# Values by Strassen's scheme, small steps of norms and attention on other engines, and a new order of work in a two-layer graph network

## The chip, the cores and the metric

The kernel runs on one core of a Trainium2 chip. The core has five engines that work side by side, each through its own queue of instructions in order: TensorE (PE; matrix products, loading its weights as PEld), VectorE (DVE), ScalarE (ACT), GpSimd (POOL) and SyncE (SP), which issues the DMA transfers here. PSUM is the small memory that TensorE writes its products to, in eight banks; SBUF is the working memory. The metric is the time of one execution on the device, in microseconds (us), lower is better, as the median of several runs.

## What is computed

Input are 64 graphs of 256 nodes with 256 features (`x`) and an integer adjacency (`adj`, 0 or 1). Two layers run one after the other on every graph:

```python
# layer 0: attention with one set of values for each of R = 4 relations, 8 heads of 32
q, k = src @ Wq + bq, src @ Wk + bk
attn = softmax(q k^T / sqrt(32))                      # per head, 256 x 256
out  = sum over r of (attn * (adj == r)) @ (src @ Wv[r] + bv[r])
x = layernorm(src + out @ Wo + bo)
x = layernorm(x + gelu(x @ W1 + b1) @ W2 + b2)        # FF = 1024

# layer 1: two graph attentions with the same adjacency
def gat(h, W, a):
    Wh = h @ W
    e = leaky_relu(Wh @ a[:256] + (Wh @ a[256:])^T, 0.2)
    return softmax(where(adj > 0, e, NEG), axis=1) @ Wh
h = layernorm(x + gat(gat(x, W1, a1), W2, a2))
return layernorm(h + relu(h @ w_ff1 + b_ff1) @ w_ff2 + b_ff2)
```

All is in float32.

## The kernel before

One graph at a time is cut into 217 named steps, built by `Graph.operations`. A name is a stage and an index: `qk`, `s`, `max`, `exp`, `rec`, `nrm` are the scores and the softmax of layer 0 (index: half m of the features, head h); `eT`, `eW`, `eR` turn the softmax round with a transpose in blocks on VectorE, a write to DRAM and a read back; `ec` copies it to PSUM on ScalarE, `pm` and `pl` multiply it by the masks of the relations on VectorE and GpSimd, `po` multiplies by the values, `oT` copies the result out of PSUM on ScalarE, `wo` is the output product and `ya` its add. `a..` and `b..` are the feed-forward blocks of the two layers: `au`/`bu` the first product, `ax`/`bx` the activation, `aS`/`bS` differences of the hidden tile, `ad`/`bd` the second product, `ae`/`be` the adds of its parts to the residual, `ag`, `ar`, `bg`, `br` the residual's gain and offset. `st`, `rt`, `nb`, `ln`, `lg`, `lb` are statistics, inverse root, offset, application, gain and shift of the four layer norms. `ga`, `gac`, `ip`, `z`, `zl`, `zm`, `zx`, `ze`, `zd`, `h1`, `h1c`, `h2`, `h2a` are the two graph attentions A and B: `ip` spreads the left scores by a transpose on TensorE, `z` adds the right ones on ScalarE while it reads PSUM, `zl` is the leaky rectifier, `zm` the mask, `zx` the maximum, `ze` the exponential, `zd` scales the rows of Wh by the softmax's sums, `h1` and `h2` are the products, `h1c` and `h2a` their readers. `hT`, `hW`, `hR`, as `aT`, `aW`, `aR` and `bT`, `bW`, `bR`, turn an activation round by way of DRAM.

Each step has a number in `PLACES`, its place. Step n of graph g is emitted at `g * PERIOD + PLACES[n]`, with PERIOD = 60, and all steps of all graphs are sorted by that number. So the places set nothing but the order in which each engine gets its instructions: graphs overlap, some seven in flight (a graph's places run from 40 to 456). Taken modulo 60, the places give the order in a steady period. The loads of the weights and the preparation of the weights have places of their own (`LOAD_PLACE`, `FFA_PLACE` and so on).

The second products of the two feed-forward blocks are done by Strassen's scheme in Winograd's form: the 2 x 2 blocks of the hidden tile and of the weights give seven products in place of eight. The combined weights are made once, by `seven_weights`; the combined left sides are the `S` steps, on GpSimd.

The values of layer 0 are not: for each half m and each half jc of the nodes, `v_product` accumulates two matmuls (k = 0, 1) of 128 x 512 (four relations of 128) in PSUM, and `v_add` (line 496) adds the bias on VectorE. A float32 matmul shows as two records in the trace.

PSUM: one tag, `mm`, with two buffers, serves nearly all products (values, qk, first products, wo, po, ga, ip, h1, h2 and three of the second feed-forward products). A new one takes the buffer whose last reader stands first in the order. The other four second products share one bank, tag `po` of pool `ps_o`; access to the same bank of a tile is ordered as emitted, reads and writes of different blocks included. Four banks hold the scores (`s`), one the copied softmax (`pe`).

The steps that the change touches, by lines: `stats` with the epsilon (341), `root` (345), `offset` (349), `residual` with its four buffers, `v_product` (489), `v_add` (496), `gat_scores` (606), `gat_leaky` (610), `gat_divide` (628 the reciprocal, 630 the scaling). Around them stand `apply` (354), `plus` and `times` (324, 321), `heads_out` (557), `difference` (400), `down` (412), `add` (420), `maximum` (510), `exponential` (518), `normalise` (528), `masked` (540), `masked_last` (545) and `gat_maximum` (617).

Of the kernel before, what the change touches and what calls it, by code (L numbers as in the profile page):

```python
# [17 lines left out]
P = 128  # L18
S = 32
A = P // S  # L20
EPS = 1e-5
# [7 lines left out]
    "load": 40.36, "cast": 58.74, "xT": 60.44, "qk0": 70, "qkc0": 71.44, "qk1": 87.85, "s0": 89.53,  # L29
    "qkc1": 91.95, "max01": 94.22, "max03": 94.25, "max02": 94.39, "exp01": 95.36, "rec01": 97.24,  # L30
    "exp03": 106.64, "exp02": 109.12, "jT": 113.27, "max00": 114.1, "exp00": 118.89, "rec02": 119.85,
    "nrm01": 120.5, "rec00": 121.94, "mask0": 122.78, "rec03": 123.27, "eT01": 124.55, "s1": 124.66,
    "mask1": 124.91, "nrm02": 125.88, "max11": 126.34, "v00": 126.75, "nrm03": 126.97, "eT02": 128.02,
    "vc00": 128.34, "nrm00": 128.91, "eW01": 131.85, "eR01": 133.5, "mask2": 134.22, "max13": 137.47,
    "eT03": 137.69, "eW02": 138.09, "max10": 139.15, "exp13": 140.04, "max12": 141.09, "eR02": 141.63,
    "v01": 142.38, "exp11": 142.41, "eT00": 142.98, "exp12": 143.77, "rec11": 143.99, "exp10": 144.12,
    "vc01": 146.63, "rec12": 146.73, "mask3": 146.81, "rec10": 147.48, "nrm11": 148.13, "eW03": 148.24,
    "ec01": 149.05, "eW00": 151.36, "rec13": 152.13, "eT11": 152.55, "nrm12": 153.62, "nrm13": 153.65,
    "eR00": 153.67, "eT12": 155.05, "v10": 155.72, "eW11": 155.83, "y": 156.64, "pm01": 156.67,
    "vc10": 157.33, "ec00": 158.45, "pl00": 159.54, "pl02": 160.62, "pm00": 161.31, "eR03": 162.29,  # L40
    "nrm10": 163.21, "ec02": 163.47, "v11": 164.04, "vc11": 164.08, "mask4": 164.38, "pm02": 164.4,
    "pl01": 165.26, "ec03": 167.13, "eT10": 167.24, "eW12": 168.06, "eR11": 169.25, "pl03": 169.3,
    "pm03": 173.29, "eR12": 174.65, "eW10": 176.2, "eT13": 176.62, "eR10": 177.38, "po0": 181.21,
    "ec11": 181.79, "oT0": 183.85, "pm11": 184.85, "ec10": 187.85, "pl10": 187.87, "pl12": 191.61,
    "pm10": 191.97, "pl11": 192.4, "yb": 193.93, "eW13": 195.61, "eR13": 196.93, "ec12": 197.13,
    "pm12": 199.06, "pl13": 199.85, "ec13": 202.51, "pm13": 205.64, "po1": 215.6, "oT1": 217.97,
    "wo": 219.51, "ya": 223.88, "st1": 228.47, "rt1": 233.65, "nb1": 233.99, "ln1": 238.78, "aT": 240.73,
    "ag": 245.39, "aW": 246.11, "ar": 246.93, "aR": 249.98, "au0": 253.28, "ax0": 255.01, "au1": 255.12,
    "ax1": 256.29, "au2": 257.32, "au3": 258.21, "ax2": 258.83, "ax3": 259.91, "ad1": 260.54, "aS1": 262.22,
    "ae1": 262.56, "ad5": 262.62, "ad2": 263.26, "aS2": 263.54, "aS3": 264.31, "ad3": 264.44, "ad7": 265.04,  # L50
    "aS4": 265.78, "ad4": 265.92, "ad6": 267.49, "ae5": 269.57, "ae7": 270.4, "ae": 270.63, "ae6": 271.84,
    "st2": 272.17, "rt2": 272.17, "nb2": 273.67, "ln2": 274.48, "lg2": 276.04, "lb2": 279.25, "hT": 280.72,
    "hW": 284.48, "hR": 287.09, "ga0": 291.2, "ga1": 292.43, "gac0": 295.5, "gac1": 295.79, "ipA": 296.6,
    "zA": 298, "zlA": 298.97, "zmA": 299.01, "zxA": 299.7, "zeA": 303.47, "zdA": 304.35, "h10": 304.89,
    "h1c0": 305.16, "h11": 306.57, "h1c1": 306.58, "ipB": 307.84, "zB": 308.32, "zlB": 309.79,
    "zmB": 309.85, "zxB": 311.38, "zeB": 311.5, "zdB": 318.17, "h2": 319.09, "h2a": 319.31, "st3": 322.4,
    "rt3": 324.85, "nb3": 325.29, "ln3": 325.64, "bT": 326.01, "bW": 326.15, "bR": 335.32, "bu0": 339.02,
    "bg": 339.45, "bx0": 339.7, "br": 344.42, "bu1": 345.17, "bx1": 346.89, "bu2": 347.56, "bx2": 348.07,
    "bS1": 349.24, "bu3": 349.7, "bd1": 350.78, "bx3": 352.33, "bS2": 355.82, "bd2": 356.22, "bd5": 356.9,
    "bd3": 357.53, "bS4": 358.73, "bd4": 360.41, "be5": 361.74, "be": 361.79, "bS3": 367.41, "bd6": 368.29,  # L60
    "be1": 372.14, "be6": 374.71, "bd7": 376.99, "be7": 378.33, "st4": 407.09, "rt4": 408.17, "nb4": 413.39,
    "ln4": 428.85, "lg4": 434.13, "lb4": 437.94, "store": 455.81,
}
LOAD_PLACE, LOAD_STEP = 62.0, 3.0
FFA_PLACE, GAT_PLACE, FFB_PLACE = 196.0, 200.0, 252.0
# [14 lines left out]
def kernel(  # L80
# [110 lines left out]
    while loads:  # L191
        issue_load()
    scale = 1.0 / math.sqrt(DH)
# [49 lines left out]
    def seven_weights(b, t):  # L243


        nc.vector.tensor_tensor(t[0], b[0][1], b[1][1], ALU.add)
        nc.vector.tensor_tensor(t[1], t[0], b[0][0], ALU.subtract)
        nc.vector.tensor_tensor(t[2], b[1][0], t[1], ALU.subtract)
        nc.vector.tensor_tensor(b[0][1], b[0][0], b[0][1], ALU.subtract)
        return {1: b[0][0], 2: b[1][0], 3: t[2], 4: b[1][1], 5: t[0], 6: t[1], 7: b[0][1]}  # L250
# [525 lines left out]
```

## Time and profile before

| | us |
|---|---|
| median of 3 runs | 3729.13 (3727.47 to 3731.34) |
| the profiled execution | 3730.06 |
| its span, first to last instruction | 3728.3 |

| engine | busy us in the span | what it does |
|---|---|---|
| TensorE | 3525.8 | 25944 matmul records |
| VectorE | 3253.6 | 5652 instructions |
| GpSimd | 2683.8 | 2246 instructions |
| ScalarE | 2476.3 | 6661 instructions |

The granted clock of TensorE is full from about 200 us on, and 0.987 over the span. DMA queues move 457.93 MB, 123 GB/s.

How to read it: busy time of an engine is the time in which one of its instructions runs, and an instruction that is held up after its start counts as busy. A record of an instruction in the timeline has its start, its length, engine, line, operation, output and input tiles, shapes and count; in square brackets the idle time of the engine in front of it and what ended it. Since the engines take their instructions in order, a wait of one instruction delays everything behind it in its queue. The chain of waits goes back from the last instruction to what released it, and so on; its pieces are in order of time, with start and length.

### The profile page before, as it was taken

The numbers are of one execution on the slowest core, as the hardware profiler recorded it, in microseconds if no ns is written. First come the engines' busy times: TensorE is split into PE (matmuls) and PEld (weight loads), VectorE is DVE, ScalarE is ACT, GpSimd is POOL, SyncE is SP. The second block draws the span as 40 slices with busy tenths as digits, with TensorE's granted clock in tenths as the row PEclk, the third lists the DMA queues.
The fourth block names the chain that finished last, engine by engine and source line by source line (L and its number), as shares of the span: only waits on it lengthen the run. The fifth ranks groups of instructions, "written<-read, shape, count | busy, mean of one in ns | idle before, by whom it ended". The sixth has DMA issues, their size and how long they took to land.

```text
span 3728.3 us, 72927 instructions
## 1 busy us (share of the span) xinstructions
PE 3525.8 (95%) x25944; PEld 2739.0 (73%) x25944; DVE 3253.6 (87%) x5652; ACT 2476.3 (66%) x6661; POOL 2683.8 (72%) x2246
## 2 busy tenths in 40 slices
PE   5899999999999999999999999999999999999986
PEld 3577777777777777777777777777777777777775
DVE  4789999999999999999999999989989989989963
ACT  4667667667667666666666666666666666666642
POOL 2577777777777777777777777777777777777753
PEclk7999999999999999999999999999999999999998
DMA  6444444444444444444444444444444444444420
GB/s 176 123 127 123 120 132 123 121 131 124 122 131 124 122 131 124 122 131 124 122 131 124 122 129 124 124 128 124 124 128 124 125 128 123 126 128 123 120 77 29
DMA packets 809883, 457.93 MB, mean 123 GB/s; under 512 B 334256, under 2 KB 718896, under 8 KB 809520
## 3 DMA queue, kind: packets, MB, share of 16 engines
q1 hardware_dynamic: 809520, 453.27, 41.5%
q8 instruction: 206, 3.38, 0.4%
q14 instruction: 157, 1.29, 0.1%
HBM read 243.42 MB, written 201.33 MB: 119 GB/s over the span
## 4 chain that ended last, share of the span: by engine, by line
PE 77%; DVE 16%; ACT 2%; DMA 2%; issue 1%; SPq 1%; POOL 0%; ACTq 0%; POOLq 0%; DVEq 0%
PE po L557 12%; PE ffb_ps L377 11%; PE v_ps L489 9%; PE ffa_ps L377 6%; PE ffa_po L412 5%; PE ffb_po L412 5%; PE ffa_pq L412 5%; PE ffb_pq L412 4%; PE s L505 4%; PE h_ps L636 4%; PE ga_wps L587 3%; PE h_ps L650 3%; DVE pm L540 3%; PE qk_ps L470 3%; PE wo_ps L577 3%; DVE gb_z L610 3%
## 5 line engine op out<-in xcount | busy, mean ns | idle before, releaser
L540 DVE TENSOR_TENSOR pm<-rel,pe 128x1536 f32<-128x1536 uint8 x512 | 886.6, 1732 | 9.8 <-ACT pe L536 7.7
L545 POOL TENSOR_TENSOR pl<-rell,eT 128x512 f32<-128x512 bf16 x512 | 589.4, 1167 | 117.9 <-DMA eT<-eT_d 98.9
L345 POOL TENSOR_TENSOR rs_x<-ve_x,nhalf 128x2 f32<-128x2 f32 x256 | 182.5, 713 | 550.4 <-DVE ve_x L341 549.9
L489 PE MATMUL v_ps<-wv,xT 128*128 128x512 f32 x1024 | 491.3, 602 | 0.4 <-DVE v L496 0.4
L518 ACT ACTIVATE e<-s,nmax 128x256 f32<-128x256 f32 x1024 | 473.1, 477 | 20.8 <-DVE nmax L510 12.7
L377 PEld LDWEIGHTS ffb_ps<-ffb_T,f 128*128 128x128 f32 x2048 | 391.3, 191 | 121.6 <-issue 71.6
L377 PE MATMUL ffb_ps<-ffb_T,f 128*128 128x256 f32 x2048 | 466.7, 381 | 13.8 <-DMA ffb_T<-ffb_T_d 13.8
L377 PE MATMUL ffa_ps<-ffa_T,w 128*128 128x256 f32 x2048 | 466.5, 381 | 1.5 <-ACT ffa_h L385 1.5
L528 ACT ACTIVATE e<-e,rden 128x256 f32<-128x256 f32 x1024 | 457.1, 507 | 8.7 <-DVE rden L523 8.7
L377 PEld LDWEIGHTS ffa_ps<-ffa_T,w 128*128 128x128 f32 x2048 | 386.4, 191 | 52.5 <-ACT ffa_h L385 2.1
L557 PE MATMUL po<-pm,v 128*32 128x256 f32 x6144 | 366.3, 385 | 18.4 <-DVE pm L540 18.4
L536 ACT COPY pe<-eT 128x512 f32<-128x512 f32 x512 | 307.0, 600 | 113.6 <-DVE rden L523 93.9
L385 ACT ACTIVATE ffb_h<-ffb_ps,bf_c 128x256 f32<-128x256 f32 x512 | 215.1, 471 | 239.2 <-PE ffb_ps L377 239.2
L296 DVE STREAM_TRANSPOSE eT_sq<-e 128x512 f32<-128x512 f32 x512 | 358.2, 700 | 12.0 <-DMA eT_d<-eT_sq 10.9
L510 DVE TENSOR_REDUCE nmax<-s 128x2 f32<-128x512 f32 x512 | 336.8, 679 | 7.2 <-PE s L505 7.2
L462 POOL TENSOR_SCALAR rel<-adT 128x512 uint8<-128x512 bf16 x192 | 310.1, 1624 | 0.0
L557 PEld LDWEIGHTS po<-pm,v 128*32 128x32 f32 x6144 | 188.5, 110 | 164.0 <-issue 25.2
L385 ACT ACTIVATE ffa_h<-ffa_ps,b_c 128x256 f32<-128x256 f32 x512 | 208.0, 473 | 144.4 <-PE ffa_ps L377 124.0
L489 PEld LDWEIGHTS v_ps<-wv,xT 128*128 128x128 f32 x1024 | 185.5, 191 | 159.6 <-issue 151.5
L400 POOL TENSOR_TENSOR ffa_t<-ffa_h,ffa_t 128x512 f32<-128x512 f32 x128 | 162.9, 1272 | 178.1 <-ACT ffa_h L385 178.1
L496 DVE TENSOR_TENSOR v<-v_ps,bv_r 128x512 f32<-128x512 f32 x256 | 173.4, 677 | 65.4 <-PE v_ps L489 65.3
L420 DVE TENSOR_TENSOR ffa_res<-ffa_po,ffa_res 128x256 f32<-128x256 f32 (+2 forms) x256 | 134.2, 524 | 91.4 <-PE ffa_po L412 86.8
(141 smaller groups left out, 8054.4 us busy)
## 6 DMA issues: line engine op xcount, KB each, us to landing
eT_d<-eT_sq SPq DMA_DIRECT2D x512, 256.0 KB, 3.1
eT<-eT_d SPq DMA_DIRECT2D x512, 256.0 KB, 2.9
xin<-in_x_dram SPq DMA_DIRECT2D x256, 64.0 KB, 3.4
adi<-in_adj_dram SPq DMA_DIRECT2D x64, 256.0 KB, 3.1
y<-in_x_dram SPq DMA_DIRECT2D x64, 256.0 KB, 4.4
ffa_T_d<-ffa_T_sq SPq DMA_DIRECT2D x64, 256.0 KB, 2.0
ffa_T<-ffa_T_d SPq DMA_DIRECT2D x64, 256.0 KB, 2.7
hT_d<-hT_sq SPq DMA_DIRECT2D x64, 256.0 KB, 3.1
```

Of the source, the lines that this page charges most:

```text
L296: nc.vector.transpose(self.sq.rearrange("p a c k y -> p (c k) a y"), src.rearrange("p c (k a x) -> p (c k) a x", k=KD, a=A))
L377: nc.tensor.matmul(p[:, f - f0, :], self.wa[:, k, f * P:(f + 1) * P], self.x.nodes(k), start=(k == 0), stop=(k == KD - 1))
L385: nc.scalar.activation(self.h[half][:, f1 + f, :], self.ps[f0][:, f, :], self.func, bias=self.ba[:, f0 + f:f0 + f + 1])
L412: nc.tensor.matmul(self.p[bank][:, k], a[:, f], seven[self.name[:3]][i][:, f], start=(f == 0), stop=(f == KF // 2 - 1))
L462: nc.gpsimd.tensor_scalar(t.rearrange("p b c k y -> p (c k) b y"), self.adT.rearrange("p c k (b y) -> p (c k) b y", b=A), float(r), None, ...
L489: nc.tensor.matmul(p, self.xT[:, k, jc * P:(jc + 1) * P], wv[:, k, m].rearrange("p r n -> p (r n)"), start=(k == 0), stop=(k == KD - 1))
L510: nc.vector.tensor_reduce(self.nmax[m, h], self.s4[m][h].rearrange("p (c n) -> p c n", c=C), AX.X, ALU.max, negate=True)
L518: nc.scalar.activation(e[:, ic, :], self.s4[m][h][:, ic * N:(ic + 1) * N], AF.Exp, bias=self.nmax[m, h][:, ic:ic + 1], accum_out=self.den[ ...
L528: nc.scalar.activation(e[:, ic, :], e[:, ic, :], AF.Copy, scale=self.rden[m, h][:, ic:ic + 1])
L540: nc.vector.tensor_tensor(self.pm[m, h], self.rel.rearrange("p r b c k y -> p r (b c k y)"), bc(self.pe[m, h], [P, R - 1, C * N]), ALU.mult)
L545: nc.gpsimd.tensor_tensor(self.pm_l[m, h], self.rel_l.rearrange("p b c k y -> p (b c k y)"), self.et[m, h].t.rearrange("p b c k y -> p (b ...
L557: nc.tensor.matmul(po[hp, :], self.v[m][:, jc, r, hp], w, start=(r == 0 and jc == 0), stop=(r == R - 1 and jc == C - 1))
```

## The change

Five things change.

1. The values go by the same seven-product scheme. The four blocks of x (two halves of the features, two of the nodes) are the left side, and four sums of them are made by a new step `xS` on VectorE. `v_weights` combines the weights once, in place. Seven products `vp1` to `vp7`, each one matmul of 128 x 512 in its own PSUM buffer, are read by `vc1` (a copy on ScalarE) and seven adds `va..` on VectorE, which build up each block from a finished one; the bias is added on GpSimd (`vb1`, `vb0`).
2. The leaky rectifier is done by ScalarE as it reads the scores from PSUM (function Prelu with slope 0.2 in place of Identity); the step `zl` is gone.
3. The row scaling of `zd` moves from VectorE to ScalarE; its reciprocal stays on VectorE.
4. In the layer norms the epsilon and the offset move from VectorE to GpSimd, as three small instructions in place of two.
5. All places are new (225 steps; a graph's places run from 23 to 371), and the residuals have three buffers in place of four.

```diff
+V_PLACE, FFA_PLACE, GAT_PLACE, FFB_PLACE = 92.0, 199.0, 202.0, 260.0
...
+    wv_t = const.tile([P, 3, R * P], F32, name="wv_t")
+    def v_weights():
+        wv_s.update(seven_weights([[wv[:, k, m].rearrange("p r n -> p (r n)") for m in range(KD)] for k in range(KD)],
+                                  [wv_t[:, i] for i in range(3)]))
...
-            self.ve = small.tile([P, C], F32, tag="ve", name=f"ve_{name}")
-            nc.vector.tensor_scalar(self.ve, self.mv[:, :, 1], EPS, None, op0=ALU.add)
         def root(self):
             self.rs = small.tile([P, C], F32, tag="rs", name=f"rs_{self.name}")
-            nc.gpsimd.tensor_tensor(self.rs, self.ve, nhalf, ALU.pow)
+            nc.gpsimd.tensor_scalar(self.rs, self.mv[:, :, 1], EPS, None, op0=ALU.add)
+            nc.gpsimd.tensor_tensor(self.rs, self.rs, nhalf, ALU.pow)
         def offset(self):
             self.nb = small.tile([P, C], F32, tag="nb", name=f"nb_{self.name}")
-            nc.vector.scalar_tensor_tensor(self.nb, self.mv[:, :, 0], -1.0, self.rs, op0=ALU.mult, op1=ALU.mult)
+            nc.gpsimd.tensor_tensor(self.nb, self.mv[:, :, 0], self.rs, ALU.mult)
+            nc.gpsimd.tensor_scalar(self.nb, self.nb, -1.0, None, op0=ALU.mult)
...
-            self.r = bp.tile([P, C, D], F32, tag="res", name=f"{self.name}_res", bufs=4)
+            self.r = bp.tile([P, C, D], F32, tag="res", name=f"{self.name}_res", bufs=3)
...
+        def x_sums(self):
+            self.xs = fp.tile([P, 4, P], F32, tag="xs", name=f"xs{self.g}", bufs=1)
+            (a11, a21), (a12, a22) = ([self.xT[:, k, c * P:(c + 1) * P] for c in range(C)] for k in range(KD))
+            t1, t2, t3, t4 = (self.xs[:, i] for i in range(4))
+            for o, t, u in ((t1, a21, a11), (t2, a22, t1), (t3, a22, a21), (t4, a12, t2)):
+                nc.vector.tensor_tensor(o, t, u, ALU.subtract)
...
-        def v_product(self, m, jc):
...
+        def v_product(self, i):
+            if i < 4:
+                k, c = ((0, 0), (1, 0), (1, 1))[i - 1]
+                a = self.xT[:, k, c * P:(c + 1) * P]
+            else:
+                a = self.xs[:, i % 4 - 1 if i > 4 else 3]
+            self.ps["v", i] = mm_tile([P, R * P], f"v_ps{self.g}_{i}")
+            nc.tensor.matmul(self.ps["v", i], a, wv_s[i], start=True, stop=True)
+        def v_sum(self, to, src, i):
+            nc.vector.tensor_tensor(self.v_part(*to), self.v_part(*src), self.ps["v", i], ALU.add)
+        def v_first(self):
+            nc.scalar.copy(self.v_part(0, 0), self.ps["v", 1])
+        def v_bias(self, m, jcs):
...
+            nc.gpsimd.tensor_tensor(v.rearrange("p c r n -> p c (r n)"), v.rearrange("p c r n -> p c (r n)"),
+                                    row.to_broadcast([P, len(range(C)[jcs]), R * P]), ALU.add)
...
-                nc.scalar.activation(self.z[:, c, :], self.ps["left"], AF.Identity,
+                nc.scalar.activation(self.z[:, c, :], self.ps["left"], AF.Prelu, alpha=ALPHA,
                                      bias=self.w[:, c, right:right + 1])
-        def gat_leaky(self):
-            nc.vector.scalar_tensor_tensor(self.z, self.z, ALPHA, self.z, op0=ALU.mult, op1=ALU.max)
...
-                nc.vector.tensor_scalar(self.w[:, c, :cols], self.w[:, c, :cols], rden[:, c:c + 1], None,
-                                        op0=ALU.mult)
+                nc.scalar.activation(self.w[:, c, :cols], self.w[:, c, :cols], AF.Copy, scale=rden[:, c:c + 1])
```

Of the new places these matter below; each is modulo 60, and the rows are the engines' orders:

| engine | part of the new order |
|---|---|
| TensorE | h2 1.6, ad2 4.1, ad3 4.9, ad4 6.9, po1 10.6, vp7 11.7, qk0 12.1, wo 15.51, vp5 15.54, s0 18.0, vp4 18.4, bu0 19.3, bu1 20.6, bu2 22.2, bu3 23.1, vp3 25.9, bd1 28.2, qk1 29.3, bd5 30.4, ga0 32.6, ga1 34.3, bd2 34.7, ipA 35.6, bd3 37.2, bd4 37.4, au0 37.7, bd6 38.0, au1 40.1, bd7 40.2, au2 40.4, au3 41.9, po0 42.8, h10 43.5, h11 46.3, ad1 49.3, vp1 50.2, ipB 50.9, ad5 52.8, ad7 53.2, vp6 54.6, s1 55.5, vp2 56.0, ad6 57.5 |
| VectorE | ae5 4.7, ae1 8.1, ae6 9.0, ae 9.4, ae7 10.4, bT 11.3, va7 12.5, va9 17.4, va5 17.5, va4 18.4, hT 21.8, aT 25.9, be5 34.9, eT13 34.9, pm00 36.2, zmA 37.2, zxA 38.1, be 38.2, be1 38.8, rec02 39.2, eT11 39.8, max03 39.87, pm03 39.89, max01 40.3, rec00 40.8, eT02 41.8, xS 42.6, eT00 42.8, zdA (reciprocal) 43.1, be6 43.5, xT 44.6, be7 46.5 |
| ScalarE | bx0 20.5, bx1 23.1, bx2 25.8, bx3 27.9, qkc1 32.7, gac0 34.2, gac1 35.0, zA 36.0, exp00 36.2, ec03 36.8, zeA 38.4, ax0 39.1, ax1 40.5, nrm02 41.3, nrm00 42.3, ax2 42.4, zdA 43.1, ax3 43.2, ec11 43.7, exp03 44.5, oT0 44.7, exp01 45.7, h1c0 47.7, h1c1 49.6, zB 51.9, vc1 53.3 |
| GpSimd | yb 1.3, nb4 1.4, aS4 1.5, pl12 3.1, lg4 4.1, rt3 4.5, nb3 7.9, lb4 9.2, mask0 9.2, vb1 12.6, pl00 13.8, rt2 15.5, nb2 15.5, mask1 16.9, lg2 19.8, lb2 19.9, rt1 20.3, nb1 22.6, pl02 23.7, bg 26.2, bS1 28.9, br 29.4, pl01 30.4, bS2 31.1, bS4 31.2, bS3 31.8, mask4 34.9, vb0 37.3, ag 39.1, pl03 39.2, mask2 40.7, mask3 43.0, aS1 44.1, aS3 46.7, aS2 48.9, pl11 50.1, pl13 52.7, cast 52.9, pl10 53.1, rt4 55.1, ar 56.1 |

Before, the same bank of the second products was used in this order: bd6 8.3, be1 12.1, be6 14.7, bd7 17.0, be7 18.3 and ad1 20.5, ad5 22.6 and ae1 22.6 (ae1 first, since equal to a tenth: 22.56 against 22.62), ad7 25.0, ad6 27.5, ae5 29.6.

## The prediction

> **What bounds the kernel now.** I read five views, in this order: the page's busy shares, the busy times by stages, the timeline of one steady period on TensorE, the chain of waits of the same period, and the timeline of VectorE beside GpSimd. The first line is the page's, the second a stretch of 560 us from the busy times by stages: length, then busy us and instruction count of PE, PEld, DVE, ACT, POOL, then granted clock, DMA share and GB/s.
>
> ```profile
> PE 3525.8 (95%) x25944; PEld 2739.0 (73%) x25944; DVE 3253.6 (87%) x5652; ACT 2476.3 (66%) x6661; POOL 2683.8 (72%) x2246
> 1560.00:2120.00 560.00, 543.24 (x4042) 423.51 (x4041) 508.79 (x881) 385.49 (x1041) 419.83 (x351) 1.00 0.43 125
> ```
>
> The heads' products of one graph (po L557 x64) start at 1987.35 and 2043.36 us in the chain: one graph takes **56.0 us**, at full clock. Of a period TensorE is busy 54.32, VectorE 50.9, ScalarE 38.5, GpSimd 42.0 us. TensorE is the bound, with 1.68 us idle a graph. The timeline says where:
>
> ```profile
> 2018.12 1.06 PE L412 MATMUL ffb_po<-f_t,ffb_t 128*128 128x128 f32 x8
> ...
> 2025.49 1.13 PE L412 MATMUL ffb_po<-f,ffb_h 128*128 128x128 f32 x8 [1.13 <-DVE ffb_res L420]
> ...
> 2034.96 1.13 PE L412 MATMUL ffa_po<-w_t,ffa_t 128*128 128x128 f32 x8 [0.54 <-DVE ffa_res L420]
> ```
>
> The two waits, 1.13 + 0.54 = 1.67 us, are all of it. In both TensorE may not write one block of a PSUM bank until VectorE has read another block of it: bd7 behind be6, ad5 behind ae1. The chain shows why be6 was late:
>
> ```profile
> 2016.35 1.72 PE v_ps L489 x4
> ...
> 2018.38 0.85 ACT gb_z L606 x2
> ...
> 2019.25 1.70 DVE gb_z L610
> ...
> 2020.97 0.81 DVE gb_z L613
> ...
> 2021.80 0.69 DVE gb_max L617
> 2022.49 1.66 DVE pm L540
> 2024.15 0.61 DVE ffb_res L420
> ```
>
> The leaky rectifier (L610) took 1.70 us; its shortest in this run is 0.69. The last view says what stretched it, and this decides the forecast:
>
> ```profile
> 2019.25 1.68 DVE L610 SCALAR_TENSOR_TENSOR gb_z<-gb_z 128x512 f32<-128x512 f32 x1 [0.46 <-ACT gb_z L606]
> 2019.12 1.27 POOL L324 TENSOR_TENSOR y<-y,bo_r 128x512 f32<-128x512 f32 x1
> 2020.34 1.73 POOL L321 TENSOR_TENSOR ffb_res<-ffb_res,gl_r 128x512 f32<-128x512 f32 x1
> 124.79 0.69 DVE L247 TENSOR_TENSOR f_t<-f_t,f 128x512 f32<-128x512 f32 x1
> 125.51 1.53 DVE L248 TENSOR_TENSOR f_t<-f,f_t 128x512 f32<-128x512 f32 x1
> 125.19 1.31 POOL L545 TENSOR_TENSOR pl<-rell,eT 128x512 f32<-128x512 bf16 x1 [3.98 <-DMA eT<-eT_d]
> ```
>
> A VectorE instruction with two SBUF inputs, begun while GpSimd works, ends a little after GpSimd's instruction does (125.19 + 1.31 = 126.50; L248 ends at 127.04), and GpSimd's next then runs long (1.73, alone 1.27). L247, begun with GpSimd idle, took 0.69. The row scaling L630 behaves alike: 0.34 at best, 0.88 on average.
>
> **The change, part by part, per graph.**
>
> *Values.* A product of 128x512 is two records; four take 1.72 us, so one record is 0.43. Eight products (16 records) become seven (14): **-0.86 us** of TensorE, on the path as TensorE is the bound. Reading the products: four adds of 0.68 (L496, 2.7 us) become seven on VectorE (4.8) and a ScalarE copy (0.6, by L536). The bias goes to GpSimd: 512 and 1024 columns at 1.27 per 512 = 3.8 us.
>
> *xS*, new on VectorE: four subtractions of 128x128, all with two SBUF inputs. By L237 (256 columns, 0.42) and L246 (512, 0.68) one costs 0.28, four in dependence X = 1.2 us if GpSimd is idle; if each waits out one GpSimd instruction of 1.3, 6.4. I work X out below.
>
> *Off VectorE:* rectifiers 1.03 + 1.60, row scaling 3.3 (110.2 + 103.3 us over 64 graphs), epsilon 1.1 (four of 273 ns), offset 2.3 (four of 586), 9.3 in all. With the values VectorE goes to 50.9 - 9.3 - 2.7 + 4.8 + X = 43.7 + X. That is no bound, and it is worth nothing by itself: TensorE's records hide it, except on the path below.
>
> *On ScalarE:* four scalings of 0.51 (L528, same shape) and the copy, 38.5 + 2.6 = 41.1 us. Prelu in place of Identity I cost at nothing: Identity, Copy and Relu run between Exps here with no load of their own (the 128 loads are the Gelu and Exp switches, two a graph, and the new places keep the Gelus together: ax0 to ax3 at 39.1 to 43.2, Exps at 38.4 and 44.5). Bounds: nothing, and four loads of 1.283.
>
> The Trainium skill ("ScalarE: Activation LUTs", Rules for kernel authors) speaks against this move: max and mul belong on VectorE, not ScalarE. The rows weigh otherwise here: 0.34 us on VectorE is met only when GpSimd is idle, and the mean of 0.88 is above ScalarE's 0.51. By the rule four scalings would lose 0.7 us, by the rows they gain 1.5; neither lies on TensorE.
>
> *On GpSimd:* twelve more instructions of 128x2. The nearest rows are a fill of 128x1 (0.10) and the power of 128x2 (0.71, L345); I take 0.2, as a tensor operation of 128x512 at 1.27 has little beside its columns. So 42.0 + 3.8 + 2.4 = 48.2 us, at most 54.4. GpSimd loses most of its slack; its order now counts.
>
> *The old waits.* In the new order be6 and be7 lie at 43.5 and 46.5 (places modulo 60) and the next writer of that bank, ad1, at 49.3; ad1, ad5, ad7, ad6 (49.3 to 57.5) all come ahead of ae5 (4.7). Both waits go: **-1.67**. What is late next? I walked TensorE's new order with the rows' durations and looked at each PSUM buffer's reader. Most readers are done 0.4 to 1 us early (bu1 behind va4, qk1 behind bx3). DMAs, as moved: hT to ga0 leaves 8.0 us for 3.1 + 3.7, bT to bu0 6.9 for 2.0 + 3.2; SP's queue stands at each read until its write has landed, with nothing urgent behind. Three res buffers suffice: the store lands some 9 us before bg needs its slot.
>
> One path is not early, **ipA to h11**. Count from the end of ipA. TensorE has bd3 and bd4 1.78, au0 1.73, bd6 0.89, au1 1.73, bd7 0.89, au2 and au3 3.46, po0 3.59, h10 0.87 = 14.94 us to h11. Meanwhile: zA 0.94; zmA 0.81, zxA 0.69, be 0.50, to 3.0; be1 waits for bd6, the same bank (1.78 + 1.73 + 0.89 = 4.4), to 5.1; two reciprocals, eT11, max03, pm03 1.65, max01, eT02 (0.60 to 0.63 each) 4.3, to 9.4; xS, X; eT00 and reciprocal 0.7. Then ScalarE in its new order: zdA 0.85, ax3 0.75, ec11 0.52, table load 1.28, exp03 0.9, oT0 0.3, hops 0.25, that is 4.85. h11 takes the PSUM buffer that oT0 reads, so it starts at 14.95 + X: **TensorE waits X.** Queued behind h11 are ad1, vp1 and ipB, so the second attention layer and the next graph's values come later by as much, and the whole period with them.
>
> What is X? xS starts at 9.4 after ipA, 38.7 us after h2 began. GpSimd, which stands last for va7 (vb1), then has mask1, gains, small steps, differences, mask4, the bias of 1024 columns, ag, pl03, mask2, mask3: by the rows aS1 runs to about 39.2. Behind it stands aS3, which waits for ax3, so xS meets idle GpSimd. X = 1.2 + a rest of 0.3 = **1.5**; between 0.8 (0.2 each) and 6.4.
>
> *Sum:* 56.0 - 0.86 - 1.67 + 1.5 = 55.0 us, 1.03 less; 63 periods give 65 us. *Ends:* the last po0 starts at 3577.31, so the drain is 151 us. From po0 to store it is 274.6 places before and 208.1 after; TensorE's work left falls from 88 to 79 us. The drain shrinks by 9 (work) to 36 (places); I take 20. The fill is led by po0 at nearly the same distance from load (141 and 139 places); four weight subtractions of 0.69 lie in it, 0 to 3 us, left out. From this execution's own 3730.1 (span 3728.3 and 1.8 around it), 0.9 above the median: 3730 - 65 - 20 = **3645**.
>
> **The rivals.**
>
> *No new wait.* If be1 is not held by bd6, or hops are shorter than I set them, the path falls below 14.9 and TensorE runs through: 53.5 us a graph, 3730 - 63 x 2.53 - 20 = 3551. For it: every other edge of the order has slack. Against: X can't be below 0.8 and the path has no slack without it.
>
> *Slower: xS behind the masks.* If GpSimd comes to mask2 only when xS starts, xS stands behind mask2 1.6, mask3 1.5 and aS1 1.3 in turn: X = 1.2 + 4.4 less some overlap, about 4.3, and 56.0 - 2.53 + 4.3 = 57.8 us a graph: 3730 + 112 - 20 = 3822. For it: L248, and GpSimd at 48 of 55 us; small steps of 0.5 instead of 0.2 put it 2 us later. Against: it waits for va7 with about 1 us to spare. It decides from X = 2.85, where 63 x (2.85 - 2.53) = 20 eats the drain's gain. GpSimd as the bound, 54.4 us and waits of 2.7 (rt3, vb1), ends as high: 3730 + 69 - 20 = 3779.
>
> *Prelu isn't where Exp is.* Then loads of 1.28 us ahead of zA and of each next Exp lie on the path: one or two more, 3645 + 81 to 162, about 3726 to 3807. Against: Relu, Copy and Identity need none.
>
> **How the numbers follow.** The wait of about 1.5 us: 0.50, its own range 3600 to 3690. No new wait: 0.22. xS behind the masks or GpSimd the bound: 0.17. Prelu's loads: 0.04. The rest, 0.07, are small waits at several buffers, between 3690 and 3730. Range **3555 to 3745**: it holds the first and last cases, most of the second, and the slower ones near X = 3. 0.2% (7.5 us) is what a measurement of this kernel tells from no change. Faster 0.76, same 0.04, slower 0.20.
>
> **What would show it.** v_ps at 896 records, 6.0 us a graph. No waits of ffb_po or ffa_po on L420. A wait of h_ps (L636) on oT, about 1.5 us; if absent, the second case. The subtractions of xS: 0.3 us each free, 1.5 behind GpSimd. GpSimd's 128x2 steps at 0.2. Still two table loads a graph. It is wrong if the period isn't 53.5 to 56, or if TensorE waits mainly elsewhere: on a DMA into bu0 or ga0, or on va4, va5 or bx3.

## The result, and the profile after

The changed kernel takes **3684.46 us** (median of 4 runs, 3676.25 to 3687.13) against 3728.95 before; the ratio is 0.9876 (95% interval 0.9864 to 0.9888). It is faster, inside the range, and 39 us slower than the 3645 forecast.

The page's first lines of the kernel after, and the same 560 us stretch of the busy times by stages as before (length; busy us and instructions of PE, PEld, DVE, ACT, POOL; granted clock, DMA share, GB/s):

```profile
span 3685.0 us, 73450 instructions
...
PE 3497.9 (95%) x25816; PEld 2749.5 (75%) x25816; DVE 2880.7 (78%) x5208; ACT 2628.1 (71%) x6981; POOL 3019.8 (82%) x3142
```

```profile
1560.00:2120.00 560.00, 545.74 (x4108) 429.75 (x4107) 454.14 (x826) 416.56 (x1110) 477.00 (x496) 1.00 0.44 128
```

TensorE is still the bound, now with GpSimd second and VectorE relieved. I count a period here from the output product (wo) of graph 5 to that of graph 63, divided by 58: 55.88 us before, **55.10 after**. TensorE's waits from 400 to 3400 us in the kernel after (total us, times, longest):

```profile
PE h_ps L664 <- ACT oT L595: 48.9, 55, 1.4
PE ga_wps L619 <- DMA hT<-hT_d: 14.0, 15, 2.7
PE ffa_ps L387 <- DMA ffa_T<-ffa_T_d: 3.2, 4, 1.6
```

The two old waits, of the second products on the adds, are gone. One new wait leads: h11 behind oT0, 0.89 us a graph. The chain of waits of one period shows the path to it (start us, length us, what):

```profile
2000.23 0.61 DVE eT_sq L306
2000.84 0.18 DVE xs L453
...
2001.04 0.36 DVE xs L453 x2
...
2001.45 0.28 DVE xs L453
2001.74 0.62 DVE eT_sq L306
2002.36 0.06 DVE ga_rden L657
...
2002.86 0.49 ACT ga_wh L659
2003.35 0.73 ACT ffa_h L395 x2
2004.08 0.49 ACT pe L568
...
2004.58 1.28 ACT L550
...
2005.88 1.02 ACT e L550 x4
2006.90 0.27 ACT oT L595
...
2007.21 1.14 PE h_ps L664 x4
```

Read downward: eT02, the subtractions xS, eT00, the reciprocal, the row scaling, ax3, ec11, the table load (the line without a name), exp03, oT0, and then TensorE may start h11.

The hT transfer was not foreseen. In the same chain, 32 us later:

```profile
2038.40 0.87 PE v_ps L511 x2
...
2039.29 3.83 DMA hT<-hT_d
...
2043.25 1.99 PE ga_wps L619 x8
```

Most of these waits begin ahead of the transfers themselves, in SyncE's queue. In 16 of the 18 graphs in which TensorE waits ahead of ga0 from 400 to 3400 us, the write was issued 1.0 to 1.9 us after its data were ready, because SyncE was still issuing the next graph's inputs; one such graph, SyncE (the inputs, then the write) and VectorE (the data, ready at 1537.51):

```profile
1536.03 2.64 SPq L178 DMA_DIRECT2D xin<-in_x_dram  x4
...
1539.44 0.41 SPq L311 DMA_DIRECT2D hT_d<-hT_sq  x1
...
1536.80 0.71 DVE L306 STREAM_TRANSPOSE hT_sq<-ffa_res 128x512 f32<-128x512 f32 x1 [0.18 <-POOL ffa_res L334]
```

### The profile page after: what moved, and what is told of

It reads as the page before. It is cut to its first block, busy times and chain, and to the rows that moved or that the text cites. A ratio compares the mean times of both kernels' runs of the same rounds, so it can differ in the third digit from the quotient of the medians.

```text
span 3685.0 us, 73450 instructions
## 1 busy us (share of the span) xinstructions
PE 3497.9 (95%) x25816; PEld 2749.5 (75%) x25816; DVE 2880.7 (78%) x5208; ACT 2628.1 (71%) x6981; POOL 3019.8 (82%) x3142
## 3 DMA queue, kind: packets, MB, share of 16 engines
q14 instruction: 165, 1.35, 0.1%
## 4 chain that ended last, share of the span: by engine, by line
PE 62%; DVE 17%; ACT 8%; DMA 6%; issue 3%; POOL 2%; SPq 2%; POOLq 0%; ACTq 0%; DVEq 0%
PE ffb_ps L387 10%; PE v_ps L511 9%; PE po L589 5%; PE ffa_po L422 5%; DVE pm L572 4%; PE ffb_pq L422 4%; PE qk_ps L487 4%; PE ffa_ps L387 4%; DVE eT_sq L306 4%; PE ffb_po L422 4%; PE ffa_pq L422 3%; PE ga_wps L619 3%; PE s L537 3%; DVE nmax L542 3%; PE h_ps L678 2%
## 5 line engine op out<-in xcount | busy, mean ns | idle before, releaser
L577 POOL TENSOR_TENSOR pl<-rell,eT 128x512 f32<-128x512 bf16 x512 | 595.9, 1170 | 15.5 <-DMA eT<-eT_d 15.2
L387 PE MATMUL ffa_ps<-ffa_T,w 128*128 128x256 f32 x2048 | 478.2, 382 | 8.9 <-ACT e L550 3.3
L387 PEld LDWEIGHTS ffb_ps<-ffb_T,f 128*128 128x128 f32 x2048 | 392.4, 192 | 102.9 <-issue 36.2
L387 PEld LDWEIGHTS ffa_ps<-ffa_T,w 128*128 128x128 f32 x2048 | 377.1, 192 | 55.3 <-ACT e L550 5.3
L589 PE MATMUL po<-pm,v 128*32 128x256 f32 x6144 | 363.7, 384 | 19.9 <-DVE pm L572 6.6
L520 DVE TENSOR_TENSOR v<-v,v_ps 128x512 f32<-128x512 f32 x448 | 298.7, 678 | 35.0 <-PE v_ps L511 32.5
L430 DVE TENSOR_TENSOR ffb_res<-ffb_po,ffb_res 128x256 f32<-128x256 f32 (+2 forms) x256 | 130.4, 509 | 240.7 <-PE ffb_po L422 134.5
L589 PEld LDWEIGHTS po<-pm,v 128*32 128x32 f32 x6144 | 206.8, 110 | 149.1 <-issue 18.2
L479 POOL TENSOR_SCALAR rel<-adT 128x512 uint8<-128x512 bf16 x192 | 289.7, 1509 | 18.8 <-DMA adT<-adb 17.6
L528 POOL TENSOR_TENSOR v<-v,bv_r 128x512 f32<-128x512 f32 (+1 forms) x128 | 232.5, 1816 | 71.5 <-DVE v L520 71.5
L410 POOL TENSOR_TENSOR ffa_h<-ffa_h,ffa_h 128x512 f32<-128x512 f32 x64 | 82.0, 1281 | 221.9 <-ACT ffa_h L395 217.5
L364 ACT ACTIVATE ffa_res<-ffa_res,nb_x,rs_x 128x256 f32<-128x256 f32 x256 | 139.9, 593 | 135.5 <-POOL nb_x L359 135.5
L550 ACT ACTIVATION_READ_ACCUMULATOR e<-s,nmax 128x1 f32 x1024 | 211.1, 206 | 0.0
```

Source lines behind the costliest of these rows:

```text
L387: nc.tensor.matmul(p[:, f - f0, :], self.wa[:, k, f * P:(f + 1) * P], self.x.nodes(k), start=(k == 0), stop=(k == KD - 1))
L550: nc.scalar.activation(e[:, ic, :], self.s4[m][h][:, ic * N:(ic + 1) * N], AF.Exp, bias=self.nmax[m, h][:, ic:ic + 1], accum_out=self.den[ ...
L577: nc.gpsimd.tensor_tensor(self.pm_l[m, h], self.rel_l.rearrange("p b c k y -> p (b c k y)"), self.et[m, h].t.rearrange("p b c k y -> p (b ...
L589: nc.tensor.matmul(po[hp, :], self.v[m][:, jc, r, hp], w, start=(r == 0 and jc == 0), stop=(r == R - 1 and jc == C - 1))
```

## The experiments

All start from the kernel after. The theory: the wait at h11 is worth what xS and exp03 put into the path ahead of oT0, so a step that only changes its place in VectorE's or ScalarE's order brings it back. Rivals are named with each run. The table has every run; "before" on the same chips was 3730.89, 3731.5 and 3731.65 us for the three groups of four.

| run | us, median (range) | ratio to before [95%] | period, us |
|---|---|---|---|
| after | 3684.46 (3676.25–3687.13) | 0.9876 [0.9864, 0.9888] | 55.10 |
| xs_behind | 3621.10 (3617.67–3625.33) | 0.9705 [0.9688, 0.9721] | 54.14 |
| xs_twice | 3777.93 (3769.17–3784.40) | 1.0127 [1.0110, 1.0143] | 56.66 |
| exp_behind | 3694.21 (3690.09–3695.53) | 0.9902 [0.9887, 0.9917] | 55.12 |
| xs_early | 3619.40 (3614.72–3624.77) | 0.9704 [0.9689, 0.9718] | 54.00 |
| xs_beside | 3745.81 (3743.18–3748.55) | 1.0039 [1.0026, 1.0052] | 56.04 |
| eight_products | 3757.91 (3754.40–3762.18) | 1.0070 [1.0055, 1.0085] | 56.02 |
| rect_scale_dve | 3872.28 (3871.24–3877.40) | 1.0375 [1.0357, 1.0392] | 58.16 |
| norms_dve | 3881.79 (3874.21–3890.41) | 1.0402 [1.0383, 1.0421] | 58.28 |
| early_load | **3604.04** (3599.39–3606.85) | **0.9658** [0.9643, 0.9672] | 53.70 |
| eight_load | 3693.25 (3689.36–3699.21) | 0.9903 [0.9887, 0.9920] | 55.09 |
| eps_dve | 3687.90 (3682.01–3689.42) | 0.9881 [0.9866, 0.9896] | 55.03 |
| rect_dve | 3755.08 (3754.44–3760.36) | 1.0067 [1.0052, 1.0082] | 56.12 |

### Is it the path through xS to h11?

**xs_behind**: the four subtractions go behind the attention's reciprocal.

```diff
-"xS": 102.642,
+"xS": 103.2,
```

> One place moved: xS from 102.642 to 103.2, that is behind zdA's reciprocal on VectorE, so that the row scaling no longer stands behind the four subtractions. Theory (the path ipA to h11 sets the wait of TensorE, and xS is a term of it): the path gets shorter by the 1.0 to 1.6 us of xS, the wait of h_ps on oT (53.2 us in the changed kernel, 0.9 us a graph) all but goes, TensorE idles 0.3 to 0.5 us a graph, the period falls from 55.16 to 54.2 to 54.5 us, the time to 3625 to 3645. Rival (ScalarE's own queue sets it: Gelus, the table load and the Exp in front of oT0 come late anyway): wait and time stay, 3675 to 3690. Second rival (another wait takes its place, at ga0 behind hT's transfer or at h2): the wait at h11 goes, but the time falls by under 20 us.

The wait of h_ps on oT falls from 48.9 us to 0.6, and the time by 63 us: 64 x 0.96 = 61 by the periods, 4 us beyond the range that was written. One number in a list of places gave more than the whole change had.

**xs_twice**: the same four subtractions, done two times over.

```diff
-for o, t, u in ((t1, a21, a11), (t2, a22, t1), (t3, a22, a21), (t4, a12, t2)):
+for o, t, u in 2 * ((t1, a21, a11), (t2, a22, t1), (t3, a22, a21), (t4, a12, t2)):
```

> The four subtractions of xS are done twice, with the same result; all places stay. Theory (xS is on the path, one to one): four more of 0.29 us in a stretch where GpSimd stands idle add 0.85 to 1.2 us to the wait of h_ps on oT and to every period: 54 to 75 us, 3740 to 3760. Rival (xS is hidden in VectorE's idle time, which is 22% of the span): no change, 3675 to 3695.

```profile
PE h_ps L664 <- ACT oT L595: 92.6, 53, 1.9
```

This wait (TensorE's waits, same window, of xs_twice) nearly doubles, to 1.75 us a graph. That is 0.86 more, as the theory has it: the added four take 0.28 or 0.29 us each, and only the first of the eight is ever held (up to 1.29 us; in after up to 1.11). But the period grows by 1.56, above what was written. The rest shows in TensorE's granted clock: 0.972 to 0.974 over the span in the four runs, against 0.983 or 0.984 in after. A line of TensorE, and the busy times by stages of the 3.4 us behind its start, with the clock of 0.50:

```profile
1997.66 1.54 PE L664 MATMUL h_ps<-ga_wh,ga_z 128*128 128x258 f32 x4 [1.95 <-ACT oT L595]
1998.30:2001.70 3.40, 3.40 (x13) 2.70 (x12) 1.83 (x2) 1.31 (x5) 3.23 (x5) 0.50 0.22 82
```

From 400 to 3400 us there are 24 such stretches, each about the end of a wait of 1.88 to 1.95 us at h11; at half speed they lose, by estimate, 24 x 1.7 = 41 us, some 0.77 a graph.

**exp_behind**: the exponential exp03 goes behind oT0 on ScalarE.

```diff
-"exp03": 104.45,
+"exp03": 104.72,
```

> One place moved: exp03 from 104.45 to 104.72, behind oT0, so that ScalarE copies the heads' product out before it loads the Exp table. Theory (the path to oT0 on ScalarE sets the wait): it gets shorter by the load of 1.28 and the Exp of 0.9 us, the wait of h_ps on oT goes altogether, the time falls by the 50 to 60 us of that wait, to 3625 to 3640; if xS alone made the wait, the two moves can't both bring it. Rival (the wait comes back 2.2 us later, since exp03 and exp01 now delay h1c0, the buffer of vp1): a wait of v_ps on ScalarE, and under 20 us gained.

```profile
PE v_ps L511 <- ACT gb_wh L670: 67.4, 55, 1.2
```

The h11 wait is gone from the list, and this one stands in its place: vp1 needs the buffer that h1c0 reads, and h1c0 now comes behind exp03 on ScalarE. The period is 55.12, as after. So the time on ScalarE can't be saved by a swap there, as the rival had it; the one on VectorE can.

### When does GpSimd hold VectorE up?

**xs_early**: xS lies ahead of the mask zmA, and there beside GpSimd's mask4.

```diff
-"xS": 102.642,
+"xS": 96.6,
```

> One place moved: xS from 102.642 to 96.6, in front of zmA, where VectorE idles 1.5 us a graph for zA; GpSimd works there without a gap (the mask of 1.5 us, then the bias of 1024 columns, 2.4 us). Theory (a VectorE instruction with two SBUF inputs waits out GpSimd's instruction in flight): each of the four subtractions waits, xS takes 4 to 6 us in place of 1.6, zmA starts 2.5 to 4.5 us late, the gain of the freed path is lost: 3680 to 3800. Rival (the subtractions cost 0.3 us wherever they stand): xS vanishes in the idle time, 3625 to 3645.

The prediction said that a VectorE instruction with two SBUF inputs, begun while GpSimd works, ends after GpSimd's does. Here are VectorE and then GpSimd in the timeline of xs_early:

```profile
2013.97 0.27 DVE L453 TENSOR_TENSOR xs<-xT 128x128 f32<-128x128 f32 x1
2014.28 0.58 DVE L453 TENSOR_TENSOR xs<-xT,xs 128x128 f32<-128x128 f32 x1
2014.79 0.28 DVE L453 TENSOR_TENSOR xs<-xT 128x128 f32<-128x128 f32 x1
2014.99 0.28 DVE L453 TENSOR_TENSOR xs<-xT,xs 128x128 f32<-128x128 f32 x1
...
2013.99 1.61 POOL L471 TENSOR_SCALAR no<-adT 128x512 uint8<-128x512 bf16 x1
```

All four subtractions end at 2015.27, within GpSimd's instruction, which ends at 2015.60 (one of them lost 0.3 us). So it is in 60 of the 64 graphs, and the time, 3619.40, lies just under the rival's 3625 to 3645, not in the theory's 3680 to 3800. The statement fell: this GpSimd instruction with one input does not hold them for its length.

**xs_beside**: xS between be and be1, beside GpSimd's vb0, ag and pl03, which have two inputs each.

```diff
-"xS": 102.642,
+"xS": 98.3,
```

> One place moved: xS from 102.642 to 98.3, between be and be1, where VectorE idles 1.6 to 2.6 us for bd6; GpSimd has tensor operations of two inputs there (bias of 1024 columns, ag, pl03), while xS in the run with place 96.6 stood beside a tensor_scalar of one input and took 1.4 us. Theory now (only a GpSimd instruction with two inputs holds VectorE's two-input instruction up for its whole length): xS takes 3 to 4.5 us, with subtractions of over 1 us in a row; the excess over the idle time delays be1 and what follows by 1 to 2 us, time 3630 to 3690. Rival (VectorE is held up only where it happens to start while the port is taken, at most once): xS under 2 us and 3615 to 3625, as at the two other places.

```profile
2024.28 0.97 DVE L453 TENSOR_TENSOR xs<-xT 128x128 f32<-128x128 f32 x1
2025.28 1.24 DVE L453 TENSOR_TENSOR xs<-xT,xs 128x128 f32<-128x128 f32 x1
2026.44 1.24 DVE L453 TENSOR_TENSOR xs<-xT 128x128 f32<-128x128 f32 x1
2027.61 0.69 DVE L453 TENSOR_TENSOR xs<-xT,xs 128x128 f32<-128x128 f32 x1
...
2022.73 2.36 POOL L528 TENSOR_TENSOR v<-v,bv_r 128x1024 f32<-128x1024 f32 x1
2025.05 1.32 POOL L331 TENSOR_TENSOR ffa_res<-y,g_r 128x512 f32<-128x512 f32 x1
2026.34 1.20 POOL L577 TENSOR_TENSOR pl<-rell,eT 128x512 f32<-128x512 bf16 x1
2027.51 1.54 POOL L479 TENSOR_SCALAR rel<-adT 128x512 uint8<-128x512 bf16 x1
```

The first three end 0.14 to 0.16 us after the bias (2025.09), the gain (2026.37) and the mask product (2027.54): one subtraction passes for each two-input instruction. The fourth, beside a one-input instruction, ends 0.75 us before it. It cost 0.69 instead of 0.28, so one input is not free, but it is no lock of its whole length. (Both one-input instructions here, L471 and L479, read bf16; whether one that reads float32 would hold is not shown.) The time is above what was expected even of this; TensorE now waits for rden (48.9 us) and for the hidden tile's activation (38.3).

The Trainium skill ("SBUF — State Buffer", Who interferes with whom) has the pair of instructions block each other fully whenever the VectorE one has two SBUF inputs and the GpSimd one reads SBUF at all. The two-input rows agree; the row of L471, which reads SBUF, does not: by that rule the second subtraction would have ended after 2015.60, and the measurement decides here.

### What each part of the change is worth

**eight_products**: the values by eight products again, at the places of vp1, vp2, vp7 and vp4; xS, the bias on GpSimd and the weights' sums are gone.

```diff
-"vp1": 110.158, "vp6": 114.571, "vp2": 116.039, "vp7": 131.698, "vp5": 135.541, "vp4": 138.406, "vp3": 145.914,
+"v00": 110.158, "v01": 116.039, "v10": 131.698, "v11": 138.406,
...
-            nc.tensor.matmul(self.ps["v", i], a, wv_s[i], start=True, stop=True)
+            for k in range(KD):
+                nc.tensor.matmul(p, self.xT[:, k, jc * P:(jc + 1) * P],
...
```

> The values by eight products again (two accumulated matmuls into each of four buffers, bias added on VectorE), at the places of vp1, vp2, vp7, vp4 and their readers; xS, the weights' combination, the copy and GpSimd's bias adds are gone, all else is as in the changed kernel. Theory (seven products take 0.86 us off TensorE, less 0.2 to 0.3 for more starts behind the scores and the heads' products, and xS at its place gives 0.9 back as a wait): records of v_ps 1024, the wait of h_ps on oT gone, period 54.2 to 54.7, time 3630 to 3665, so faster than the changed kernel by 20 to 55 us. Rival (the seven products bring their 0.86 us in full, and the wait at h11 comes from the norms, the scaling or the order): 55.7 to 56 us a graph, 3715 to 3740.

A miss: 3757.91, not 3630 to 3665; TensorE waits 36.9 us for hT there, and the next two runs show what is left without that. **eight_load** moves the transfers of the next graph's inputs in it, **early_load** in xs_early, behind the reads of hT and ffa_T:

```diff
-"load": 23.357,
+"load": 35.1,
```

> eight_products with the inputs' transfers issued behind the reads of hT and ffa_T. It leaves open in eight_products how much of its 3758 us is TensorE's own work and how much the waits for hT (36.9 us in 53 graphs). Counted from start to start, TensorE works 55.20 us a graph there and 53.73 in the kernel after the change. Theory (the seven products save 1.47 us a graph of TensorE in these places, the rest of the loss is the transfer): 64 x 0.6 = 40 us or less are won, 3710 to 3735, and it doesn't come below 3700. Rival (the waits for hT come from VectorE's eight evictions ahead of the squares): 3745 to 3765.

> The subtractions at 96.6 as in xs_early, and the five transfers of the next graph's inputs issued behind the reads of hT and ffa_T (place 35.1) instead of ahead of the write of hT (23.4). Theory (what is left of TensorE's waiting in xs_early is the hT transfers, 7.3 us of labelled waits in 3000 us and a mean period of 54.09 against the shortest of 53.7, and it comes from the inputs' bytes ahead of them): the write of hT takes under 3 us, the waits for hT vanish, 3595 to 3612 us. Rival (the hT waits come from a late squares step on VectorE and not from the bytes ahead): no change, 3615 to 3625. Second rival: the inputs arrive late for the transposes or delay the writes of eT behind them: above 3625.

The DMA issues from 400 to 3400 us (KB, median us from issue to landing) of after and of early_load, and all of TensorE's waits in early_load:

```profile
hT_d<-hT_sq SPq DMA_DIRECT2D x54, 256.0 KB, 3.2
```

```profile
hT_d<-hT_sq SPq DMA_DIRECT2D x56, 256.0 KB, 2.0
```

```profile
PE po L589 <- ACT ffa_h L395: 0.4, 1, 0.4
PE h_ps L664 <- ACT oT L595: 0.4, 2, 0.2
PE ffb_ps L387 <- DMA ffb_T<-ffb_T_d: 0.2, 1, 0.2
```

The write of hT is issued 0.03 us after its data are ready and lands in 2.0 us instead of 3.2: it neither stands behind the issue of five transfers nor shares the DMA engines with their 512 KB (how much each is worth was not separated). TensorE runs through: 53.70 us a period and 3604.04 us, as expected, the best kernel of this study. In eight_load the same move wins 65 us, more than the 40 written and past the floor of 3700: beside the waits for hT (36.9 us in the 3000) those for ffa_T, oT and other tiles went too, from 52.7 us of labelled waits in all to 3.9, which is 0.9 us a graph of the 1.0.

These two kernels have next to no waits, so their difference is TensorE's work: 3693.25 - 3604.04 = 89 us, 1.39 a graph. Counted from start to start in TensorE's timeline, waits left out, one graph takes 54.34 us before, 53.73 after and in early_load, 55.10 in eight_load. Seven products in place of eight save **1.37 us in the new order**, with the eight at these places (values 7.18 to 6.52 us, the other 0.7 in pieces of 0.1 to 0.2 about the scores, the graph attention's and the second products and wo, whose cause I did not settle), but the new order by itself costs 0.76 of TensorE's time, so 0.61 is left.

**rect_scale_dve** puts the leaky rectifier (right ahead of the mask) and the row scaling back on VectorE; **rect_dve** the rectifier alone.

```diff
-nc.scalar.activation(self.z[:, c, :], self.ps["left"], AF.Prelu, alpha=ALPHA,
+nc.scalar.activation(self.z[:, c, :], self.ps["left"], AF.Identity,
...
+nc.vector.scalar_tensor_tensor(self.z, self.z, ALPHA, self.z, op0=ALU.mult, op1=ALU.max)
...
-nc.scalar.activation(self.w[:, c, :cols], self.w[:, c, :cols], AF.Copy, scale=rden[:, c:c + 1])
+nc.vector.tensor_scalar(self.w[:, c, :cols], self.w[:, c, :cols], rden[:, c:c + 1], None, op0=ALU.mult)
```

> Leaky rectifier and row scaling back on VectorE (Identity on ScalarE, then the rectifier right in front of the mask; two scalings behind the reciprocal), all else as in the changed kernel. Theory (both lie on the path ipA to h11): the rectifier adds 0.7 to 1.7 us in front of zmA, by what GpSimd has in flight, while the scaling's 0.85 us on ScalarE turns into 0.7 to 1.7 on VectorE, off ScalarE's queue: the wait of h_ps on oT grows by 0.3 to 1.5 us, time 3700 to 3780. Rival (VectorE has 22% of its time free, so it is hidden): 3675 to 3690.

> Only the leaky rectifier is back on VectorE, right ahead of the mask; the row scaling stays on ScalarE. In rect_scale_dve the rectifier took 1.69 us for ga_z and 1.18 for gb_z (0.69 where GpSimd ran no two-input instruction), the scaling 0.68 to 0.86 a piece. Theory (the rectifier lies on the path from ipA to h11, whose wait ends last): +1.0 to +1.7 us a graph, 3745 to 3800, the larger part of the 187 us of both. Rival (the scaling, which releases h1 itself, carries the loss): 3685 to 3730.

Both together cost 188 us, above what was expected. The timeline of rect_scale_dve, one VectorE line (two instructions) and then two GpSimd lines:

```profile
2045.65 2.28 DVE L662 TENSOR_SCALAR ga_wh<-ga_wh,ga_rden 128x258 f32<-128x258 f32 x2
...
2045.20 1.27 POOL L410 TENSOR_TENSOR ffa_h<-ffa_h,ffa_h 128x512 f32<-128x512 f32 x1 [1.14 <-ACT ffa_h L395]
2046.44 1.33 POOL L410 TENSOR_TENSOR ffa_t<-ffa_h,ffa_t 128x512 f32<-128x512 f32 x1
```

The two row scalings, 0.34 each at best, took 2.28 us: they have one tensor input, and stand until GpSimd's two instructions end, at 2047.77. This is so for every one that begins while GpSimd runs a two-input instruction of over 1 us: 99 of them took 0.53 to 1.38 us, the 107 others at most 0.36. TensorE waits for the scaling itself ahead of h2 (39.8 us in the 3000). On ScalarE the same scaling takes 0.49 to 0.52 us in every one of 220 cases. Of the 188 us the rectifier brings 71 (rect_dve, inside what the theory wrote), so the scaling with what it sets off is the larger part, against that expectation. Nor did the rectifier's loss come by the place the theory named: h_ps waits 43.3 us for oT, as in after, and a wait of the first hidden product on an add (17.8 us) and many small unlabelled ones make it up.

**norms_dve** puts epsilon and offset of the norms back on VectorE, **eps_dve** epsilon alone.

```diff
+nc.vector.tensor_scalar(self.ve, self.mv[:, :, 1], EPS, None, op0=ALU.add)
...
-nc.gpsimd.tensor_tensor(self.nb, self.mv[:, :, 0], self.rs, ALU.mult)
-nc.gpsimd.tensor_scalar(self.nb, self.nb, -1.0, None, op0=ALU.mult)
+nc.vector.scalar_tensor_tensor(self.nb, self.mv[:, :, 0], -1.0, self.rs, op0=ALU.mult, op1=ALU.mult)
```

> Epsilon and offset of the norms back on VectorE, two small instructions in place of three on GpSimd, all else as in the changed kernel. Theory (no norm is on the path ipA to h11, and the small steps move only GpSimd's slack): 3675 to 3695, the wait at h11 the same 0.9 us within 0.3; GpSimd 2 to 3 us a graph less busy. Rival (GpSimd's order sets when aS1 and with it xS run, so that GpSimd earlier by 1 to 2 us frees xS, or VectorE held up by GpSimd at the offset costs up to 0.6 us on four norms): beyond 15 us either way.

> Only epsilon is added on VectorE, right behind the statistics; the offset stays on GpSimd, so VectorE never waits for GpSimd's power. Theory (norms_dve's loss is VectorE standing in order for GpSimd's power, 1.24 us a graph, and its 128x2 product of two inputs being held by a GpSimd instruction, 0.47 instead of some 0.15 us, four times): epsilon alone costs only what its own four steps are held, 4 x 0.4 = 1.6 us of VectorE that mostly lies off the path: 3685 to 3745. Rival (any 128x2 step on VectorE in this order costs by being held): half of the 197 us or more, above 3775.

norms_dve loses 197 us where under 15 were expected; eps_dve loses nothing that can be measured (3687.90), though its epsilon steps are held too (0.55 us in the median, 0.17 at best): the wait at h11 falls to 21.8 us, and small waits elsewhere make it up. So the loss is the offset's, by subtraction (alone it was not run). The timeline of norms_dve, GpSimd and then VectorE:

```profile
2011.09 0.70 POOL L356 TENSOR_TENSOR rs_x<-ve_x,nhalf 128x2 f32<-128x2 f32 x1 [1.45 <-DVE ve_x L352]
2011.75 1.28 POOL L334 TENSOR_TENSOR ffb_res<-ffb_res,bl_r 128x512 f32<-128x512 f32 x1
...
2011.82 1.23 DVE L360 SCALAR_TENSOR_TENSOR nb_x<-mv_x,rs_x 128x2 f32<-128x2 f32 x1 [0.42 <-POOL rs_x L356]
```

The moment GpSimd finishes the power it begins a two-input instruction; VectorE, which waited in order for the power, begins its offset 0.07 us later and stands behind that instruction: 1.23 us for a 128x2 product whose shortest was 0.15. The hand-over makes the collision. A graph loses 1.2 us of VectorE's time by the wait for the power and 1.7 by the hold of its four offsets; which of the two carries the 197 us was not separated. With the offset on GpSimd behind the power, VectorE neither waits nor is held.

## Why the prediction was right, and where it was not

*The bound, the old waits, the new wait.* Right. The two waits of 1.67 us are gone, and h11 behind oT0 through xS, eT00, the scaling, ax3, ec11, the load and exp03 is the leading wait in their place; xs_behind and xs_twice show the cause.

*X.* Right in the sum: 1.5 predicted, 1.59 measured (101.5 us of xS in 64 graphs; from the first start to the last end 1.48 on average). Its two parts, 1.2 free and a rest of 0.3, were 0.98 and 0.50, so their errors nearly cancel. And GpSimd was seldom idle, which the sum had assumed: in 44 of 63 graphs the first subtraction begins while aS1 runs and stands until it ends, as here (VectorE, GpSimd):

```profile
2109.85 1.07 DVE L453 TENSOR_TENSOR xs<-xT 128x128 f32<-128x128 f32 x1
...
2109.49 1.28 POOL L410 TENSOR_TENSOR ffa_t<-ffa_h 128x512 f32<-128x512 f32 x1
```

The wait came to 0.89 all the same, because TensorE's work from ipA to h11 is 15.5 us, not 14.94: au3 ahead of the heads' products and h10 behind them take 0.27 longer each than the rows I took them from.

*The records.* 896 v_ps records, as predicted, but 6.52 us a graph and not 6.0; -0.86 was mis-sized, it is -0.61. In TensorE's timeline of after:

```profile
2011.95 1.02 PE L511 MATMUL v_ps<-wv_t,xs 128*128 128x512 f32 x2
2012.90 1.15 PE L537 MATMUL s<-kT,qT 32*128 32x256 f32 x16
```

From its start to the next start a product of two records takes 0.86 us among full products, and 0.95 (as here) to 0.97 beside the scores or heads' products, which use a part of the array; that holds for five of the seven products. The Trainium skill ("TensorEngine Tiling (Array Packing)", Key Properties) says that a change of the tiling mode drains TensorE; the rows fit that, with 0.1 to 0.27 us a change, but no run here varied it alone.

*The transfers.* Wrong: hT had "8.0 us for 3.1 + 3.7". The sum counts from issue to landing and leaves out the time that the write stands in SyncE's queue, 1.0 to 1.9 us in the graphs that wait, behind the inputs that the new order issues just ahead of it (before it was 1.35 us, with 1.5 to spare at ga0). In 2 of the 18 the write was issued 0.2 us after its data and took 4.0 and 4.2; in the two longest waits, 2.5 and 2.7 us, it was late and took over 5. Together 0.26 us a graph. early_load shows that the place of the inputs makes it.

*The ends, -20 us.* **This step failed.** By its own count, from the last po0 to the end, the drain fell from 151.0 to 140.9 us, 10 and not 20. The fill, left out at 0 to 3, took more than that back: po0 of graph 5 starts at 344.75 us, against 329.26 before, with 1914 records of TensorE ahead of it against 1878. Work left the drain for the fill, and I counted one side only. Counted by wo, the ends give nothing: from start to the wo of graph 5 it is 370.12 us before and 370.10 after, from the last wo to the end 117.3 and 118.8. (TensorE's granted clock, all but full between, is down to 0.87 and 0.83 from the last wo on.) So the 43 us between the two profiled spans are 58 x 0.77 = 45 from the steady part, less 1.5 from the ends, where I had 65 + 20.

*The period.* That 55.10 came so near to 55.0 is partly luck: errors cancel. TensorE's work is 53.73 where 53.47 was forecast, the wait at h11 0.89 where it was 1.5, and other waits 0.48 where there were none. The mean period before was 55.88, not the 56.0 of the one I read, so the gain is 0.77 and not 1.03.

*The placements.* The small GpSimd steps at 0.2 us and two table loads a graph are right (groups of after: count, busy us, mean ns, idle):

```profile
L359 POOL TENSOR_SCALAR nb_x<-nb_x 128x2 f32<-128x2 f32 x256 | 62.7, 245 | 22.4
L395 ACT ACT_TABLE_LOAD x64 | 82.1, 1283 | 0.3
L550 ACT ACT_TABLE_LOAD x62 | 79.5, 1283 | 1.1
```

But "worth nothing by itself" for VectorE's relief was wrong in the new order: taking back the rectifier and the scaling costs 188 us, the norms' steps 197 (the epsilon alone next to nothing).

*The rivals.* "No new wait" (3551) was the kernel with xS placed elsewhere; even early_load stays at 3604, mostly since its 53.70 us of work are not 53.5 and its ends give nothing. "xS behind the masks" didn't occur, and its price was wrong: I charged mask2 and mask3 in full, and a one-input GpSimd instruction doesn't hold xS so. With two-input instructions beside it, xs_beside, it came out slower than before, as that rival feared. Prelu needed no table load.

## What to carry to other kernels

When a change swaps one leading wait for another, walk the new chain and try each step on it at another place of its engine's order before judging the change: moving four 0.28 us instructions, and five transfers from ahead of an urgent write to behind it, won 80 us here, the change itself 44. A saving at the ends counts only if fill and drain are both summed. Small float32 steps on SBUF data were safest here on ScalarE or on the GpSimd queue that makes their input, not on VectorE just behind a GpSimd result.

## What the hardware showed unexpectedly

A VectorE instruction with one tensor input from SBUF was held like those with two (row scaling 2.28 us for two instead of 0.68) until a two-input GpSimd instruction ended, while a one-input GpSimd instruction (bf16 in) delayed the subtractions by 0.3 to 0.4 us only. VectorE's adds out of PSUM, its block transposes and its maxima kept 0.65 to 0.72 us beside two-input GpSimd instructions in rect_scale_dve.

A wait of TensorE near 2 us cost more than itself. In all the profiles here, from 400 to 3400 us, the granted clock fell to a half for 3.4 us at a time 31 times, each time about the end of a wait of 1.88 us or more (24 in xs_twice; two in after, about the hT waits of 2.5 and 2.7 us), and not once about a shorter one; 12 waits of 1.88 us or more passed without it.
